# A graph layer's gather, split between GpSimd and TensorE: six instead of five of sixteen columns by matmul, with the nodes in ten sets of 625 instead of seven of 896

## The chip, the core and the metric

The kernel runs on one core of a Trainium2 chip. The metric is the device time in microseconds (us), as the median of three runs. Engines are named as in the profile: PE (TensorE; PEld is its weight load), DVE (VectorE), ACT (ScalarE), POOL (GpSimd), SP (SyncE, which issues most DMAs).

## What is computed

The layer has 6250 nodes of 64 features and 206250 edges, sorted by destination. Everything is float32.

```python
h = jnp.maximum(_layernorm(x), 0.0)
msg = relu(h[src] + edge_attr)                 # 206250 x 64
agg = segment_sum(msg, dst, num_segments=6250)
h = h + agg
h = relu(h @ W1 + b1)
return x + (h @ W2 + b2)
```

The expensive part is `h[src]`: 206250 rows of 256 bytes are picked by number.

## The kernel before

**Groups.** The edges are worked off in 201 groups of 1024 and a tail (g = 0 to 201). A group is a tile of 128 partitions by 8 columns; each column is 128 edges. For a group, `load` (L170) fetches the edge attributes `ea` by a DMA from SP's queue and the rows `xg` by one indirect DMA per column from POOL's queue (`gather`, L158). Groups 0 to 3 gather from `x` and normalise on the spot (`norm_edges`); the others gather from `h_rows`, the normalised rows that the kernel first writes to DRAM. The tiles `ea` and `xg` have `LOOK` = 10 buffers each, so group g uses the buffer of group g - 10 and its gathers wait until that group's rows have been added.

`messages` (L459) adds `xg` to `full`, a PSUM tile into which ACT has copied `ea` (`take`, L450), and applies relu on ACT (L469). `one_hot` (L437) compares destinations with slots of a window of 48 nodes on DVE, `window_sum` (L472) sums messages by destination on PE (16 matmuls in the profile for a group), and `sum_into_z` (L433) adds the sum to `z` on DVE, two groups later. Every 512 finished nodes, `hidden`, `result` and `store` apply the two dense layers, with the `rows` banks of PSUM in between.

**Columns by TensorE.** In 98 pairs of groups (k = 2 to 99, groups 2k and 2k + 1) POOL does not gather all 16 columns: the last `EVEN` = 3 columns of the even group and the last `ODD` = 2 of the odd one are gathered by matmul. The node numbers are cut into `SB` = 7 sets of `PART` = 896 nodes, each of `BB` = 7 blocks of `BN` = 128. Before the pairs begin, `ranks` (L244) gives each edge of these columns its set (`part`), its number in the set (`node`) and a slot of 128 in the set (`place`), by masks, matmuls and DVE passes for each set. For one pair, the work is:

- `hold`, `mask` (L330, L337; DVE) and `source` (L346): `T` = 5 matmuls turn this into rows that say which node stands in which slot. ACT casts them (L353), SP writes them to DRAM and reads them back as a broadcast to all partitions (`sources`, L357, 224 KB). `spot` (L359) loads the slots of the pair's edges as a broadcast (`spots`, L362).
- `find` (L365; DVE, L370): one comparison for each block makes `found`, one-hot weights from nodes to slots, 7 passes of 896 elements.
- `slots_of` (L381; PE, L386) looks the nodes up: for each set 7 matmuls of 192 columns against `hp`, the node rows in three bfloat16 pieces. Two sets share one `rows` bank. `slots_out` (L393; ACT, L394) casts them to `picked`.
- `back` (L373; DVE, L378): for each set a comparison makes `backs`, one-hot weights from slots to edges, 7 passes of 640 elements.
- `room` (L396; ACT, L403) copies the edge attributes of two columns into a `pick` bank, and `pick` (L406; PE, L412) adds to each column 7 matmuls of 192 columns, one for each set. `messages` then sums pieces and attribute (DVE, L466).

**Order.** It is written out by hand in `half(g)` (L526); each engine works its own queue in this order. In the even half of pair k, PE does for pair k + 1 the lookup of sets 0 and 1, the source matmuls of pair k + 2, the window sum of group g - 1, the lookup of sets 2 and 3 and the pick of the odd group; DVE does the messages of g, `back(k + 1)` and `mask(k + 3)`. In the odd half PE does the lookups of sets 4 to 6, the window sum, and the pick of the next even group; DVE does the messages, `find(k + 2)` and `hold(k + 3)`. ACT's order in the odd half is: cast of sets 4 and 5, relu of the messages, attributes of the next group, cast of set 6, attributes into the `pick` banks. `rows`, `pick` and `full` have two PSUM banks each.

At group 8, `find_left` looks once for edges that did not fit; a loop for them at the end of the kernel is not entered here.

Of the kernel before, what the change touches and what calls it, by code (L numbers as in the profile page):

```python
# [35 lines left out]
TN = N - NB * P * R  # L36
XC = 3
EPS = 1e-5
LOOK = 10
AHEAD = 6  # L40
LAG = 2
AB = 4


SB, BB, BN = 7, 7, 128
KB = SB * BB
PART = BB * BN
EVEN, ODD = 3, 2
T = EVEN + ODD
K0, K1 = 2, NG // 2  # L50
KS = K1 - K0
# [9 lines left out]
def kernel(  # L61
# [17 lines left out]
    const = ctx.enter_context(tc.tile_pool(name="const", bufs=1))  # L79
    edge = ctx.enter_context(tc.tile_pool(name="edge", bufs=LOOK))  # L80
    work = ctx.enter_context(tc.tile_pool(name="work", bufs=2))
# [255 lines left out]
    def mask(k):  # L337

        at = hot.tile([P, T, SB], F16, name="at", bufs=1)
        nc.vector.tensor_tensor(at, part[:, k - K0].unsqueeze(2).to_broadcast([P, T, SB]),  # L340
                                of_part.unsqueeze(1).to_broadcast([P, T, SB]), ALU.is_equal)
        mk = hot.tile([P, T, SB], F16, name="mask")
        nc.vector.tensor_tensor(mk, at, node[:, k - K0].unsqueeze(2).to_broadcast([P, T, SB]), ALU.mult)  # L343
        masks[k] = mk

    def source(k):  # L346

        oh, mk = holds.pop(k), masks.pop(k)
        ps = psum.tile([SB, P], F32, name="rows", bufs=2)
        for t in range(T):  # L350
            nc.tensor.matmul(ps, mk[:, t, :], oh[:, t, :], start=(t == 0), stop=(t == T - 1))  # L351
        col = hot.tile([SB, P], I16, name="source")
        nc.scalar.copy(col, ps)  # L353
        line = dram.tile([SB, P], I16, name="source_row", bufs=3)
        nc.sync.dma_start(out=line, in_=col)
        sources[k] = hot.tile([P, SB * P], I16, name="sources")
        nc.sync.dma_start(out=sources[k], in_=line.rearrange("(o m) s -> o (m s)", o=1).to_broadcast([P, SB * P]))  # L357

    def spot(k):  # L359

        spots[k] = hot.tile([P, T * P], BF16, name="spots")
        nc.sync.dma_start(out=spots[k], in_=spot_rows[(k - K0) * T:(k - K0 + 1) * T, :]  # L362
                          .rearrange("(o t) s -> o (t s)", o=1).to_broadcast([P, T * P]))

    def find(k):  # L365

        row = sources.pop(k)
        found[k] = hot.tile([P, BB, SB, P], BF16, name="found")
        for b in range(BB):
            nc.vector.tensor_scalar(found[k][:BN, b].rearrange("p m s -> p (m s)"), row[:BN], nodes_of[:BN, b:b + 1], None,  # L370
                                    op0=ALU.is_equal)

    def back(k):  # L373

        row = spots.pop(k).bitcast(I16)
        backs[k] = hot.tile([P, SB, T, P], BF16, name="backs")
        for m in range(SB):
            nc.vector.tensor_scalar(backs[k][:, m].rearrange("p t s -> p (t s)"), row, ids[:, m:m + 1], None,  # L378
                                    op0=ALU.is_equal)

    def slots_of(k, m, n):  # L381

        ps = psum.tile([P, 2, 3 * D], F32, name="rows", bufs=2)
        for i in range(n):
            for b in range(BB):
                nc.tensor.matmul(ps[:, i], found[k][:BN, b, m + i, :],  # L386
                                 hp[:BN, (m + i) * BB + b].rearrange("p t d -> p (t d)"),
                                 start=(b == 0), stop=(b == BB - 1))
        if m == 0:
            picked[k] = hot.tile([P, SB, 3 * D], BF16, name="picked")  # L390
        halves[k, m] = ps[:, :n]

    def slots_out(k, m, n):  # L393
        nc.scalar.copy(picked[k][:, m:m + n], halves.pop((k, m)))  # L394

    def room(g):  # L396

        m = pool_cols(g) if g < NG else G
        _, _, ea, pks = taken[g]
        for i in range(0, G - m, 2):  # L400
            n = min(2, G - m - i)
            pk = psum.tile([P, 2, 4, D], F32, name="pick", bufs=2)
            nc.scalar.copy(pk[:, :n, 3], ea[:, m + i:m + i + n])  # L403
            pks.append((pk, i, n))

    def pick(g):  # L406

        k, t0 = g // 2, EVEN if g % 2 else 0
        for pk, i, n in taken[g][3]:
            for u in range(n):  # L410
                for m in range(SB):
                    nc.tensor.matmul(pk[:, u, :3].rearrange("p t d -> p (t d)"), backs[k][:, m, t0 + i + u, :],  # L412
                                     picked[k][:, m], start=(m == 0), stop=(m == SB - 1))
# [19 lines left out]
    def sum_into_z(g):  # L433
        at = window_start(g)
        nc.vector.tensor_tensor(z[:, ds(at, W)], z[:, ds(at, W)], aggs.pop(g), ALU.add)  # L435
# [9 lines left out]
    def enter(g):  # L445
        if g <= NG and g not in taken:
            ea, xg = loaded[g] if g < RAW else load(g)
            taken[g] = [None, xg, ea, []]

    def take(g):  # L450

        if g <= NG:
            enter(g)
            n = pool_cols(g)
            full = psum.tile([P, G, D], F32, name="full", bufs=2)
            nc.scalar.copy(full[:, :n], taken[g][2][:, :n])  # L456
            taken[g][0] = full

    def messages(g):  # L459
        n, m = (G, pool_cols(g)) if g < NG else (CT, CT)  # L460
        full, xg, _, pks = taken.pop(g)
        if g < RAW:
            norm_edges(xg)
        nc.vector.tensor_tensor(full[:, :m], full[:, :m], xg[:, :m], ALU.add)  # L464
        for pk, i, c in pks:
            nc.vector.tensor_reduce(full[:, m + i:m + i + c], pk[:, :c].rearrange("p j t d -> p j d t"),  # L466
                                    AX.X, ALU.add)
        msg = work.tile([P, G, D], F32, name="msg", bufs=3)
        nc.scalar.activation(msg[:, :n], full[:, :n], AF.Relu)  # L469
        msgs[g] = msg  # L470

    def window_sum(g):  # L472
        n, oh, msg = G if g < NG else CT, hots.pop(g), msgs.pop(g)
        if g % AB == 0:
            banks.append(psum.tile([D, AB, W], F32, name="agg", bufs=1))
        pa = banks[-1][:, g % AB]
        for j in range(n):
            nc.tensor.matmul(pa, msg[:, j, :], oh[:, j, :], start=(j == 0), stop=(j == n - 1))  # L478
        aggs[g] = pa
# [34 lines left out]
    def blocks_behind(g):  # L514
        for c in sorted(res):
            store(c, *res.pop(c))
        for c in sorted(hid):
            res[c] = result(c, *hid.pop(c))
        for c in range(NB):
            if READY[c] == g:  # L520
                hid[c] = hidden(c)

    def is_set(k):
        return K0 <= k < K1

    def half(g, groups=True, sets=True):  # L526

        k, even = g // 2, g % 2 == 0
        now = sets and is_set(k + 1)
        first = (((0, 2),) if even else ((4, 2),)) if now else ()  # L530
        if groups:
            enter(g + AHEAD)
        for c in first:
            slots_of(k + 1, *c)
        if even and sets:
            if is_set(k + 2):
                source(k + 2)
            if is_set(k + 3):
                spot(k + 3)
        for c in first:  # L540
            slots_out(k + 1, *c)
        if groups:
            if g >= LAG:
                sum_into_z(g - LAG)
                blocks_behind(g - LAG)
            messages(g)
        if now and not even:
            slots_of(k + 1, 6, 1)
        if groups:
            take(g + 1)  # L550
        if now and not even:
            slots_out(k + 1, 6, 1)
        ahead = sets and g < NG and is_set((g + 1) // 2)
        if ahead:
            room(g + 1)
        if groups and g >= 1:
            window_sum(g - 1)
        if now and even:
            slots_of(k + 1, 2, 2)
            slots_out(k + 1, 2, 2)  # L560
        if ahead:
            pick(g + 1)
        if even:
            if now:
                back(k + 1)
            if sets and is_set(k + 3):
                mask(k + 3)
        elif sets:
            if is_set(k + 2):
                find(k + 2)  # L570
            if is_set(k + 3):
                hold(k + 3)
        if groups:
            one_hot(g)
        if g == 8:
            find_left()

    heads, rows = [], []
    with tc.tile_pool(name="rank", bufs=1) as rank:
# [28 lines left out]
        for g in range(2 * K0):  # L608
            half(g, sets=False)
# [36 lines left out]
    for g in range(2 * K0):  # L646
        half(g, groups=False)
    for g in range(2 * K0, NG + 1):
        half(g)
# [81 lines left out]
```

## Time and profile before

| | us |
|---|---|
| median of 3 runs (1465.42 to 1466.75) | 1465.74 |
| the profiled execution | 1465.74 |
| its span, first to last instruction | 1464.0 |
| PE busy | 1126.0 (77%) |
| PE's weight loads busy | 1029.1 (70%) |
| DVE busy | 1042.1 (71%) |
| ACT busy | 452.1 (31%) |
| POOL busy | 1103.6 (75%) |

The profile shows one execution. A group of instructions is one line, engine, operation and shape, with its count, its busy time, the mean of one and the idle time of the engine just ahead of it, with what ended that. A mean can be longer than busy time divided by the count, because one instruction starts while the one ahead of it ends; where the text counts "start to start" it goes by the first. The mean clock granted to PE is 0.881 of full speed. The DMA engines moved 140.35 MB, 96 GB/s on average. In the timeline, a line merges like instructions in a row (x21) and shows in brackets how long the engine stood idle before and what ended it.

### The profile page before, as it was taken

To read this page: it belongs to the slowest core of one execution; us is meant where nothing else is said; L and a number is where in the kernel's file an instruction comes from. 1 tells how busy PE (TensorE), PEld (TensorE's weight loads), DVE (VectorE), ACT (ScalarE), POOL (GpSimd) and SP (SyncE) were. 2 spreads that over 40 slices of the span, in tenths; PEclk is the share of its full clock that TensorE was granted. 3 is DMA by queue.
4 is the path that set the end of the run, shared out by engine and by line. 5 is a ranking of instruction groups with operands and counts; after the bars stand their busy time and mean duration, and the time that the engine had idled before them with its cause. 6 is when DMAs were issued, how large, how long until landed. Compare 5 with 4: busy or idle time off the path is not lost. (4 is left out here: it accounts for less than half of the span.)

```text
span 1464.0 us, 32135 instructions
## 1 busy us (share of the span) xinstructions
PE 1126.0 (77%) x12197; PEld 1029.1 (70%) x12197; DVE 1042.1 (71%) x2734; ACT 452.1 (31%) x1257; POOL 1103.6 (75%) x1133
## 2 busy tenths in 40 slices
PE   2419799988877886878788788787778887877874
PEld 1308788877767776777777777677767776776773
DVE  6658998986667676676776767677677676766752
ACT  3323343432232332223233232222323233223231
POOL 7777777777777777777777777777777777777774
PEclk9759999998898898888899899989999889889885
DMA  5523444543342334334343343434334334333321
GB/s 172 122 44 97 100 126 111 124 114 80 100 109 77 103 89 98 98 86 101 83 106 90 94 106 82 102 88 99 90 91 109 95 87 107 84 95 92 95 66 25
DMA packets 110196, 140.35 MB, mean 96 GB/s; under 512 B 34740, under 2 KB 66100, under 8 KB 110036
## 3 DMA queue, kind: packets, MB, share of 16 engines
q1 hardware_dynamic: 72884, 99.71, 24.5%
q0 software_dynamic: 35904, 36.84, 12.8%
q8 instruction: 97, 1.59, 0.4%
q10 hardware_dynamic: 1248, 1.70, 0.3%
q14 instruction: 63, 0.52, 0.1%
HBM read 134.64 MB, written 3.50 MB: 94 GB/s over the span
## 5 line engine op out<-in xcount | busy, mean ns | idle before, releaser
L160 POOL DMA_INDIRECT xg<-h_rows,src_sb x1090 | 1068.8, 981 | 334.1 <-issue 274.9
L412 PE MATMUL pick<-picked,backs 128*128 128x192 bf16 x3430 | 389.2, 279 | 226.9 <-ACT pick L403 226.7
L412 PEld LDWEIGHTS <-backs 128*128 128x128 bf16 x3430 | 346.1, 111 | 243.0 <-issue 224.9
L386 PE MATMUL rows<-hp,found 128*128 128x192 bf16 x4802 | 482.6, 257 | 7.1 <-DVE found L370 5.5
L386 PEld LDWEIGHTS <-found 128*128 128x128 bf16 x4802 | 422.3, 102 | 25.7 <-DVE found L370 10.7
L464 DVE TENSOR_TENSOR full<-full,xg 128x320 f32<-128x320 f32 (+1 forms) x202 | 106.9, 529 | 278.3 <-DMA xg<-h_rows,src_sb 212.0
L370 DVE TENSOR_SCALAR found<-sources,nodes_of 128x896 bf16<-128x896 int16 x686 | 260.5, 451 | 37.3 <-DMA sources<-source_row 37.3
L394 ACT CAST picked<-rows 128x384 bf16<-128x384 f32 (+1 forms) x392 | 171.0, 436 | 243.2 <-PE rows L386 243.1
L478 PE MATMUL agg<-oh,msg 128*64 128x48 f32 x3224 | 232.8, 227 | 13.6 <-ACT msg L469 8.1
L478 PEld LDWEIGHTS agg<-oh,msg 128*64 128x64 f32 x3224 | 207.4, 140 | 47.3 <-issue 25.8
L378 DVE TENSOR_SCALAR backs<-spots,ids 128x640 bf16<-128x640 int16 x686 | 222.2, 393 | 0.0
L466 DVE TENSOR_REDUCE full<-pick 128x128 f32<-128x512 f32 (+1 forms) x294 | 179.6, 611 | 50.4 <-PE pick L412 12.9
L469 ACT ACTIVATE msg<-full 128x512 f32<-128x512 f32 x202 | 119.6, 592 | 245.4 <-DVE full L466 225.2
L353 ACT CAST source<-rows 7x128 int16<-7x128 f32 x98 | 24.9, 254 | 439.9 <-PE rows L351 435.7
L440 DVE TENSOR_TENSOR oh<-slot,wslots 128x384 f32<-128x384 int16 x202 | 110.1, 545 | 0.0
L456 ACT COPY full<-ea 128x320 f32<-128x320 f32 (+1 forms) x202 | 92.5, 458 | 0.0
L333 DVE TENSOR_TENSOR holds<-place,wslots 128x640 f16<-128x640 f32 x98 | 79.6, 813 | 5.6 <-DMA spot_rows<-sp 5.6
L403 ACT COPY pick<-ea 128x128 f32<-128x128 f32 (+1 forms) x294 | 66.8, 256 | 0.0
L351 PE MATMUL rows<-holds,mask 128*7 128x128 f16 x490 | 44.1, 222 | 5.7 <-DVE mask L343 5.7
L435 DVE TENSOR_TENSOR z<-z,agg 64x48 f32 x202 | 38.3, 190 | 8.4 <-PE agg L478 5.2
L351 PEld LDWEIGHTS <-mask 128*7 128x7 f16 x490 | 25.9, 87 | 22.8 <-issue 14.8
L160 POOL DMA_INDIRECT xg<-in_x_dram,src_sb x32 | 32.9, 1028 | 11.0 <-issue 9.4
(101 smaller groups left out, 254.4 us busy)
## 6 DMA issues: line engine op xcount, KB each, us to landing
ea<-in_edge_attr_dram SPq DMA_DIRECT2D x201, 256.0 KB
sources<-source_row SPq DMA_DIRECT2D x98, 224.0 KB
xg<-h_rows,src_sb POOLq DMA_INDIRECT x1090
spots<-spot_rows SPq DMA_DIRECT2D x98, 160.0 KB
source_row<-source SPq DMA_DIRECT2D x98, 1.8 KB
x_sb<-in_x_dram SPq DMA_DIRECT2D x4, 384.0 KB
h_rows<-ln_h SPq DMA_DIRECT2D x4, 384.0 KB
h_nodes<-h_rows SPq DMA_DIRECT2D x2, 768.0 KB
```

The source lines that it names most:

```text
L160: nc.gpsimd.indirect_dma_start(out=xg[:, j, :], out_offset=None, in_=rows[:, :], in_offset=bass.IndirectOffsetOnAxis(ap=idx[:, j:j + 1], a ...
L370: nc.vector.tensor_scalar(found[k][:BN, b].rearrange("p m s -> p (m s)"), row[:BN], nodes_of[:BN, b:b + 1], None, op0=ALU.is_equal)
L378: nc.vector.tensor_scalar(backs[k][:, m].rearrange("p t s -> p (t s)"), row, ids[:, m:m + 1], None, op0=ALU.is_equal)
L386: nc.tensor.matmul(ps[:, i], found[k][:BN, b, m + i, :], hp[:BN, (m + i) * BB + b].rearrange("p t d -> p (t d)"), start=(b == 0), stop=(b ...
L394: nc.scalar.copy(picked[k][:, m:m + n], halves.pop((k, m)))
L412: nc.tensor.matmul(pk[:, u, :3].rearrange("p t d -> p (t d)"), backs[k][:, m, t0 + i + u, :], picked[k][:, m], start=(m == 0), stop=(m == ...
L440: nc.vector.tensor_tensor(oh[:, :n], slot[:, cols_of(g)].unsqueeze(2).to_broadcast([P, n, W]), wslots[:, :W].unsqueeze(1).to_broadcast([P, ...
L456: nc.scalar.copy(full[:, :n], taken[g][2][:, :n])
L464: nc.vector.tensor_tensor(full[:, :m], full[:, :m], xg[:, :m], ALU.add)
L466: nc.vector.tensor_reduce(full[:, m + i:m + i + c], pk[:, :c].rearrange("p j t d -> p j d t"), AX.X, ALU.add)
L469: nc.scalar.activation(msg[:, :n], full[:, :n], AF.Relu)
L478: nc.tensor.matmul(pa, msg[:, j, :], oh[:, j, :], start=(j == 0), stop=(j == n - 1))
```

## The change

Six of sixteen columns go by TensorE, in place of five: four of the even group and two of the odd one. The nodes are cut into ten sets of 625 (five blocks of 125) in place of seven of 896 (seven blocks of 128). So `find` makes 5 passes of 1280 elements over 125 partitions, `back` 10 passes of 768; `slots_of` does 50 matmuls, with 125 rows contracted; a column's pick has 10 matmuls; `source` has 6. POOL gathers 10 columns for a pair in place of 11. The even group's picks fill two `pick` banks, and ACT's casts are five of two sets each. In the odd half the lookups of sets 4 and 5 and of sets 6 and 7 both come first, and that of sets 8 and 9 behind the messages. The buffers of `ea` and `xg` go from 10 to 9.

```diff
-LOOK = 10
+LOOK = 9
...
-SB, BB, BN = 7, 7, 128
+SB, BB, BN = 10, 5, 125
 KB = SB * BB
 PART = BB * BN
-EVEN, ODD = 3, 2
+EVEN, ODD = 4, 2
 T = EVEN + ODD
...
         now = sets and is_set(k + 1)
-        first = (((0, 2),) if even else ((4, 2),)) if now else ()
+        first = (((0, 2),) if even else ((4, 2), (6, 2))) if now else ()
...
         if now and not even:
-            slots_of(k + 1, 6, 1)
+            slots_of(k + 1, 8, 2)
         if groups:
             take(g + 1)
         if now and not even:
-            slots_out(k + 1, 6, 1)
+            slots_out(k + 1, 8, 2)
```

## The prediction

> **What bounds the kernel now.** I read the groups of instructions first, then busy time in stretches, then the waits, then single instructions of one stretch.
>
> The group of gathers on POOL, from the page:
>
> ```profile
> L160 POOL DMA_INDIRECT xg<-h_rows,src_sb x1090 | 1068.8, 981 | 334.1 <-issue 274.9
> ```
>
> 981 ns busy and 334.1/1090 = 306 ns idle before each: POOL never waits longer than its own issue, and 1090 x 1.287 = 1403 us of 1464 are this one queue. Busy time in two stretches, early and the rest (columns: length, busy us of PE, PEld, DVE, ACT, POOL with counts, granted clock, DMA share, GB/s):
>
> ```profile
> 160.00:200.00 40.00, 38.75 (x486) 36.68 (x485) 38.28 (x105) 16.93 (x48) 30.55 (x32) 1.00 0.50 119
> 309.00:1447.00 1138.00, 904.42 (x9792) 832.86 (x9792) 787.79 (x2092) 339.37 (x980) 866.81 (x890) 0.88 0.37 93
> ```
>
> From 160 to 200 us PE is 97% busy and DVE 96%, at clock 1.00: compute is working off gathers that POOL had laid up, and a pair of groups takes 10.0 us (start to start of the messages of every second group: 161.96, 172.02, 182.01, 192.05, 202.06). After 309 us PE is 79% busy, and the waits from 400 to 1400 us say for what:
>
> ```profile
> POOL xg L160 <- issue: 194.2, 637, 0.3
> ...
> DVE full L464 <- DMA xg<-h_rows,src_sb: 170.8, 55, 6.3
> ```
>
> DVE waits for gathered rows; POOL waits for nobody. So a pair costs 11 gathers x 1.28 = 14.1 us, though compute could do it in 10.0. The compute-bound stretch is thus the measure of what the new kernel can do. One pair of it on PE, with the ACT steps ahead of its end:
>
> ```profile
> 240.40 1.89 PE L412 MATMUL pick<-picked,backs 128*128 128x192 bf16 x21 [0.49 <-ACT pick L403]
> ...
> 242.13 1.32 PE L386 MATMUL rows<-hp,found 128*128 128x192 bf16 x14
> ...
> 243.38 0.44 PE L351 MATMUL rows<-holds,mask 128*7 128x128 f16 x5
> ...
> 243.75 1.13 PE L478 MATMUL agg<-oh,msg 128*64 128x48 f32 x16
> ...
> 244.82 1.33 PE L386 MATMUL rows<-hp,found 128*128 128x192 bf16 x14
> ...
> 245.98 1.32 PE L412 MATMUL pick<-picked,backs 128*128 128x192 bf16 x14
> ...
> 247.14 1.90 PE L386 MATMUL rows<-hp,found 128*128 128x192 bf16 x21
> ...
> 248.49 0.48 ACT L394 CAST picked<-rows 128x384 bf16<-128x384 f32 x1 [1.83 <-PE rows L386]
> 248.96 1.13 PE L478 MATMUL agg<-oh,msg 128*64 128x48 f32 x16
> 248.99 0.60 ACT L469 ACTIVATE msg<-full 128x512 f32<-128x512 f32 x1
> ...
> 250.38 1.89 PE L412 MATMUL pick<-picked,backs 128*128 128x192 bf16 x21 [0.28 <-ACT pick L403]
> ```
>
> Start to start, 14 matmuls of 192 columns take 1.16 us: 83 ns each. The pair ends with a short wait (0.28) for ACT.
>
> **POOL, less.** One column of each pair goes to TensorE: 98 gathers fewer, 98 x 1.28 = 126 us. Alone this would give 1464 - 126 = 1338. It can't all be kept, for two reasons that follow.
>
> **PE, more.** Picks go from 35 (5 columns x 7 sets) to 60 (6 x 10), set lookups from 49 to 50, source matmuls from 5 to 6. I rebuild the pair above from its own pieces. Pick of the even group: 1.73 + 19 x 0.083 = 3.31. Lookup of two sets: 1.25 - 4 x 0.083 = 0.92. Source: 0.37 + 0.07 = 0.44; sums 1.07; lookup of two more 0.83; pick of the odd group 1.16 + 6 x 0.083 = 1.66. Then three lookups of two sets 2.49 + 0.07 and sums 1.07. Without waits: 8.23 + 3.63 = 11.86.
>
> Two waits for ACT, whose order the edit keeps. First, the pick of the odd group waits for its bank: source copy, cast, message, copy of attributes, copy into the bank. The same chain runs above from the source matmul (243.38); without a pause its steps are 0.54 + 0.16 + 0.48 + 0.50 + 0.40 + 0.44 = 2.52, while PE now has 0.44 + 1.07 + 0.83 = 2.34 to do: 0.18 of wait. Second, in the odd half an extra cast (sets 6 and 7) stands ahead of the message. The pick of the odd group ends at T; that lookup ends at T + 1.66; cast at + 0.19, message + 0.50, attributes + 0.49, cast of sets 8 and 9 + 0.31, bank + 0.42, pick + 0.33: T + 3.90, where PE is ready at T + 3.63: 0.27. A pair is 11.86 + 0.18 + 0.27 = 12.31.
>
> Real pairs also carry the output blocks: from 161.96 to 308.71 us 14 pairs took 146.75, or 10.48, against 10.0 undisturbed, about 0.1 of that a wait for broadcast sources. I add 0.4: **12.7 us per pair**.
>
> **DVE beside it.** Start to start before: found 0.379 each, backs 0.306, so 0.073 for 256 elements. After: 5 found of 1280 cost 0.46 to 0.48 each (2.35, was 2.65), 10 backs of 768 0.335 each (3.35, was 2.14); holds + 0.13; reductions + 0.27 (a full second bank instead of a half one); the smaller add - 0.07; masks + 0.05. From 9.6 to 10.9 of 12.7: covered, with 1.8 to spare. If that cover went, each further us per pair is 98 us.
>
> **DMA.** Broadcast sources grow from 224 to 320 KB a pair. They landed 3.3 to 4.1 us after issue; by size alone 0.6 to 1.0 more. DVE wants them 5.4 us after the source matmul, and copy, write and issue take 2.8 of it: found starts up to 2 us late. DVE's spare 1.8 and 1.2 us before its reductions hold up ACT hide it, barely; bounds 0 and 1.0 per pair, I take 0. Spots (160 to 192 KB) are loaded a half pair ahead: nothing.
>
> **POOL against DVE.** Gathers beside found lasted 1.06 us on average, beside backs 0.953, otherwise 0.94. Longer found passes: 0 to 0.05 per gather, 0 to 50 us of POOL's time, which no longer sets the end; I take 0.
> The Trainium skill (SBUF — State Buffer, Who interferes with whom) says that VectorE in a two-port mode and GpSimd exclude one another for a whole instruction. It speaks against this change, which lengthens that work; the found rows agree in kind (+ 0.12), the backs rows hardly (+ 0.01). By the rule, with every gather delayed by half a longer instruction, the sum would rise by 948 x 0.2 = 190 us on POOL, an estimate I don't use.
>
> **The start.** DVE ranks 10 sets instead of 7 (six more pairs of 0.88, fourteen pairs 0.10 longer, three masks and some passes of 588 instead of 490 elements: 9.3 us, of which 1 to 2 fall in DVE's gaps), and a fifth chunk of spots is stored (+ 1.0; 97.98 to 98.98 before). Message of group 4: 123.54 becomes about 133. POOL: before, its next gather never waited, though at 123.22 it needed the buffer just freed by group 4 (ten buffers). Now nine buffers hold groups up to 12, 44 gathers after 49.3 us, so POOL stands from about 106 to 131. Bounds: 0 to 30 us; it matters only if POOL is the bound again. Once, at group 8, DVE's pass over leftovers cost 8 us (156.37 where 148.4 was due); it stays.
>
> **The sum.** 133 + 8 + 98 x 12.7 + 13 (from the message of group 200 to the end; 16.4 before with its waits for gathers) = **1399** of span. The profiled execution took 1465.74, which is the median, for a span of 1464.0: + 1.7, so **1400 us**.
>
> **Rivals.**
> *POOL stays the bound* (20%): ACT's two waits are not there and a pair takes 12.3 or less. Then 131 + 948 gathers x 1.284 + 15 = 1363, + up to 8 from group 8: about 1370 (1355 to 1380). For: the waits are sums of short steps. Against: PE's work alone is 11.86 + 0.4.
> *Late sources stretch DVE* (18%): 0.5 to 0.7 more per pair, 1449 to 1467, say 1455. For: 25 waits for them already, 37.3 us in total. Against: DVE's spare time.
> *Slower: the 125-row lookups* (12%). The 50 lookups of a pair load weights of 125 rows instead of 128. No row shows that shape. The transposes' load of 106 columns took 170 ns, the full ones about 100; if the new loads did likewise, 50 x 0.087 = 4.3 us per pair: 1400 + 426 = 1826. It decides from 0.7 us per pair, 14 ns per lookup. Against: a load of 106 rows (group L221) took 110 ns, a full one of its kind 90 to 148. Nor does a busier PE look throttled: clock 1.00 at 97% busy.
> The Trainium skill (TensorE: Matmul & The Clock Gate, LDWEIGHTS) says that loading goes by columns, not rows; no run here shows 125 rows.
> *The forecast* has 50%, own range 1380 to 1430. That the edit does something else is no rival: the instruction order of the changed kernel shows 992 gathers from h_rows and found passes of 125x1280.
>
> **Range and chances.** 1358 to 1460 takes in the forecast, the POOL case and the smaller half of late sources; about 2 in 10 is outside. Faster by over 0.2% (what a measurement of this kernel can tell) 0.84, within 0.03, slower 0.13: the 125-row case and the far end of late sources.
>
> **What would show it.** Right: in mid-kernel PE 93% busy or more, clock near 1.00, POOL now waiting for L464 to free buffers, message to message of a pair 12.3 to 13, L403 ending PE's short waits. Wrong: gathers still at 1.28 start to start with no pause (POOL), L370 waiting for sources in most pairs (late sources), lookups over 90 ns apart (125 rows), DVE near 100%.

## The result and the profile after

The changed kernel takes 1385.93 us (median of 4 runs, 1383.09 to 1387.15) against 1466.12 for the kernel before: ratio 0.945, 95% interval 0.9434 to 0.9467. The forecast was 1400 in a range of 1358 to 1460. The profiled execution took 1385.12 us, its span is 1383.3.

The gathers on POOL, from the page, and busy time in two stretches (columns as in the prediction):

```profile
L160 POOL DMA_INDIRECT xg<-h_rows,src_sb x992 | 987.2, 995 | 334.4 <-issue 264.3
```

```profile
300.00:1200.00 900.00, 887.18 (x10871) 838.62 (x10869) 818.53 (x1987) 350.63 (x966) 688.49 (x695) 1.00 0.43 115
1200.00:1369.00 169.00, 146.49 (x1791) 137.77 (x1788) 129.82 (x312) 58.41 (x158) 129.07 (x132) 0.97 0.37 94
```

From 300 to 1200 us PE is 98.6% busy (887.18 of 900) at clock 1.00: compute sets the pace. After 1200 us PE falls to 87%. The waits from 200 to 1180 us and from 1180 to 1369 us (total, times, longest) say why:

```profile
DVE full L466 <- PE pick L412: 29.8, 52, 1.0
DVE found L370 <- DMA sources<-source_row: 27.4, 25, 2.2
```

```profile
DVE full L464 <- DMA xg<-h_rows,src_sb: 16.5, 8, 4.6
PE pick L412 <- ACT pick L403: 11.0, 8, 2.5
...
DVE full L464 <- issue: 8.9, 2, 8.1
```

At first DVE waits for PE's picks, never over 1.0 us, and for sources, never over 2.2; at the end it waits for gathered rows again, as all through the kernel before. (The 8.1 us put down to "issue" stand ahead of the addition of group 200, at 1366.11; before, the same wait, 8.1 as well, is put down to the rows.) POOL, meanwhile, stood still once, at the start. Its timeline, with its last gather:

```profile
110.47 0.94 POOL L160 DMA_INDIRECT xg<-h_rows,src_sb  x1 [0.30 <-issue]
137.35 0.94 POOL L160 DMA_INDIRECT xg<-h_rows,src_sb  x1 [25.93 <-DVE full L464]
...
1368.29 0.94 POOL L160 DMA_INDIRECT xg<-h_rows,src_sb  x1 [0.30 <-issue]
```

Up to 110.47 us POOL has gathered groups 4 to 12, all that nine buffers hold. The addition of group 4 frees one at 137. From there 948 gathers follow one another at 1.30 us, no two starts more than 3.4 apart, until the last starts at 1368.29; 15.0 us later the kernel ends. POOL's lead, from the start of a group's last gather to the addition of its rows, shrinks all the while: 50 us for group 18, 22 for group 102, 4 for group 172 (at about 1190 us). So there are two chains: PE's, which sets the pairs until about 1200 us, and POOL's, which uses up its lead by then and sets the end.

One undisturbed pair on PE, with ACT's steps ahead of its two picks:

```profile
707.83 3.46 PE L412 MATMUL pick<-picked,backs 128*128 128x192 bf16 x40
...
711.13 0.99 PE L386 MATMUL rows<-hp,found 125*128 125x192 bf16 x10
...
712.05 0.50 PE L351 MATMUL rows<-holds,mask 128*10 128x128 f16 x6
...
712.48 1.13 PE L478 MATMUL agg<-oh,msg 128*64 128x48 f32 x16
712.58 0.26 ACT L353 CAST source<-rows 10x128 int16<-10x128 f32 x1 [4.61 <-PE rows L351]
712.75 0.46 ACT L394 CAST picked<-rows 128x384 bf16<-128x384 f32 x1
...
713.12 0.58 ACT L469 ACTIVATE msg<-full 128x512 f32<-128x512 f32 x1
...
713.54 1.00 PE L386 MATMUL rows<-hp,found 125*128 125x192 bf16 x10
713.61 0.47 ACT L456 COPY full<-ea 128x384 f32<-128x384 f32 x1
714.02 0.25 ACT L403 COPY pick<-ea 128x128 f32<-128x128 f32 x1
...
714.38 1.81 PE L412 MATMUL pick<-picked,backs 128*128 128x192 bf16 x20
...
716.03 2.64 PE L386 MATMUL rows<-hp,found 125*128 125x192 bf16 x30
...
717.05 0.48 ACT L394 CAST picked<-rows 128x384 bf16<-128x384 f32 x1 [2.00 <-PE rows L386]
...
717.88 0.48 ACT L394 CAST picked<-rows 128x384 bf16<-128x384 f32 x1 [0.34 <-PE rows L386]
718.26 0.60 ACT L469 ACTIVATE msg<-full 128x512 f32<-128x512 f32 x1
...
718.60 1.13 PE L478 MATMUL agg<-oh,msg 128*64 128x48 f32 x16
...
718.75 0.39 ACT L456 COPY full<-ea 128x256 f32<-128x256 f32 x1
719.05 0.49 ACT L394 CAST picked<-rows 128x384 bf16<-128x384 f32 x1
719.42 0.48 ACT L403 COPY pick<-ea 128x128 f32<-128x128 f32 x2
...
719.76 0.41 PE L412 MATMUL pick<-picked,backs 128*128 128x192 bf16 x3
```

The next pick starts at 719.76, 11.93 us after the first (the view ends at 720 and shows three of its matmuls). No bracket stands at any PE line; brackets show waits over 0.15 us, so PE hardly waited.

### The profile page after: what moved, and what is told of

It is laid out like the page before. It is cut to its first block, busy times and chain, and to the rows that moved or that the text cites. A ratio compares the mean times of both kernels' runs of the same rounds, so it can differ in the third digit from the quotient of the medians.

```text
span 1383.3 us, 37550 instructions
## 1 busy us (share of the span) xinstructions
PE 1242.3 (90%) x14894; PEld 1163.1 (84%) x14894; DVE 1185.2 (86%) x2847; ACT 508.4 (37%) x1356; POOL 1022.5 (74%) x1035
## 4 chain that ended last, share of the span: by engine, by line
PE 61%; DMA 8%; POOL 8%; DVE 6%; issue 5%; ACT 2%; DVEq 0%; POOLq 0%; SPq 0%; ACTq 0%
PE pick L412 27%; PE rows L386 21%; PE agg L478 10%; POOL xg L160 8%; DMA xg<-h_rows,src_sb 5%; PE rows L351 2%; DVE backs L378 2%; DVE full L466 1%; DVE found L370 1%; DMA sources<-source_row 1%; PE rows L499 1%; ACT picked L394 1%; PE rows L486 1%; DMA spots<-spot_rows 1%; ACT full L456 1%
## 5 line engine op out<-in xcount | busy, mean ns | idle before, releaser
L412 PE MATMUL pick<-picked,backs 128*128 128x192 bf16 x5880 | 517.1, 246 | 23.5 <-ACT pick L403 20.7
L412 PEld LDWEIGHTS <-backs 128*128 128x128 bf16 x5880 | 488.9, 98 | 28.2 <-issue 21.4
L386 PE MATMUL rows<-hp,found 125*128 125x192 bf16 x4900 | 459.8, 247 | 6.5 <-DVE found L370 5.7
L386 PEld LDWEIGHTS <-found 125*128 125x128 bf16 x4900 | 404.8, 98 | 18.3 <-DVE found L370 7.4
L378 DVE TENSOR_SCALAR backs<-spots,ids 128x768 bf16<-128x768 int16 x980 | 335.5, 415 | 0.0
L394 ACT CAST picked<-rows 128x384 bf16<-128x384 f32 x490 | 234.3, 478 | 274.2 <-PE rows L386 269.4
L370 DVE TENSOR_SCALAR found<-sources,nodes_of 125x1280 bf16<-125x1280 int16 x490 | 251.0, 577 | 38.0 <-DMA sources<-source_row 37.6
L466 DVE TENSOR_REDUCE full<-pick 128x128 f32<-128x512 f32 x294 | 205.7, 700 | 67.5 <-PE pick L412 36.0
L464 DVE TENSOR_TENSOR full<-full,xg 128x256 f32<-128x256 f32 (+1 forms) x202 | 99.1, 491 | 33.4 <-DMA xg<-h_rows,src_sb 22.8
L333 DVE TENSOR_TENSOR holds<-place,wslots 128x768 f16<-128x768 f32 x98 | 92.4, 943 | 6.0 <-DMA spot_rows<-sp 6.0
```

Of the source, the lines that this page charges most:

```text
L386: nc.tensor.matmul(ps[:, i], found[k][:BN, b, m + i, :], hp[:BN, (m + i) * BB + b].rearrange("p t d -> p (t d)"), start=(b == 0), stop=(b ...
```

## The experiments

All times are medians; "before" is 1466.1 to 1466.6 in each comparison.

| run | what differs from the changed kernel | us | ratio to before, 95% interval |
|---|---|---|---|
| (changed) | | 1385.93 | 0.945, 0.9434 to 0.9467 |
| pick9 | PE: 6 of a pair's 60 pick matmuls left out | 1382.83 | 0.9426, 0.9411 to 0.944 |
| gather9 | POOL: 9 gathers a pair in place of 10 | 1362.61 | 0.9295, 0.928 to 0.9309 |
| look8 | 8 buffers in place of 9 | 1393.42 | 0.9504, 0.9491 to 0.9517 |
| xg11 | 11 buffers for rows, 7 for attributes | 1374.89 | 0.937, 0.9357 to 0.9383 |
| cols5 | ten sets, but 5 columns | 1480.21 | 1.0092, 1.0076 to 1.0107 |
| sets7 | 6 columns, but seven sets | 1373.36 | 0.9368, 0.9354 to 0.9382 |
| nodes2 | node loads cut in two | 1381.39 | 0.942, 0.9407 to 0.9433 |
| k0_4 | TensorE's columns from group 8 on | 1376.28 | 0.9389, 0.9376 to 0.9402 |
| cols7 | 7 columns, seven buffers | 1444.65 | 0.9846, 0.9831 to 0.9861 |
| best | nodes2, and 13 buffers for rows, 5 for attributes | 1358.83 | 0.9262, 0.9249 to 0.9274 |

**Which chain ends last: pick9 and gather9.** The first takes work from PE alone:

```diff
-                for m in range(SB):
+                for m in range(SB - 1):
                     nc.tensor.matmul(pk[:, u, :3]..., picked[k][:, m], start=(m == 0),
-                                     stop=(m == SB - 1))
+                                     stop=(m == SB - 2))
```

> Leaves out one of the ten matmuls of each pick (the tenth set), so 588 PE matmuls fewer, 6 a pair or 0.5 us a pair; POOL's gathers are as before. Theory (two chains that end almost together; POOL's ends last: from 137 us on, where group 4 frees a buffer, 948 gathers follow one another at 1.297 us, and 14 us follow the last): 1380 to 1387, because POOL's chain is untouched. Rival 1 (PE alone sets the end): 98 x 0.5 = 49 us less, about 1337.

Measured: 1382.83, 3 us less, not 49. The shorter work is there: many pairs take 11.4 us in place of 11.93. But POOL's last gather comes at 1366.2 (1368.3 in the changed kernel), and in the waits from 900 to 1369 us DVE now waits for rows much earlier:

```profile
DVE full L464 <- DMA xg<-h_rows,src_sb: 33.5, 19, 3.7
```

From the messages of group 10 to those of group 100 a pair takes 11.93 in the mean, and from there to group 200 12.91, close to POOL's ten gathers (10 x 1.295): a faster PE only meets POOL's chain sooner. So PE alone does not set the end. The second takes work from POOL alone:

```diff
+        n = pool_cols(g)
+        if g % 2 and n < G and g < NG:
+            n -= 1
+            nc.sync.dma_start(out=xg[:, n, :], in_=h_rows[g:g + P, :])
-        gather(xg, src_sb[:, cols_of(g)], pool_cols(g), x if g < RAW else h_rows)
+        gather(xg, src_sb[:, cols_of(g)], n, x if g < RAW else h_rows)
```

> In each pair one of the ten columns that POOL gathers is filled by a plain DMA of 128 neighbouring rows from SP's queue instead, with rows that are not the edge's, so POOL has 9 gathers a pair (98 x 1.297 = 127 us less) and PE the same work. Theory (two chains that end almost together): the PE chain shows alone: 139 + 8 + 98 x 12.3 to 12.4 + 13 = 1365 to 1376, so 10 to 20 us less than the changed kernel and no more. Rival 1 (PE alone sets the end): 1386, no change. Rival 2 (POOL alone): 1386 - 127 = 1259.

Measured: 1362.61, 23 us less and not 127, a little below the range given. PE's chain shows alone now: POOL starts its last gather at 1314.0, 47 us before the end, and waits for DVE to free buffers (from 300 to 1200 us; lines are 4 further down in this kernel):

```profile
POOL xg L160 <- DVE full L468: 75.6, 96, 2.4
```

From the messages of group 4 (139.3) to those of group 200 (1347.7), less the 8 us at group 8, a pair takes 12.25 us. PE's chain is thus 139.3 + 8 + 98 x 12.25 + 13.2 = 1361 of span, and POOL's, 1383, ends 22 us behind it.

**POOL's standstill: look8 and xg11.** The first is `LOOK = 8`; the second deals the 18 buffers out anew:

```diff
-        ea = edge.tile([P, G, D], F32, name="ea")
+        ea = edge.tile([P, G, D], F32, name="ea", bufs=LOOK - 2)
-        xg = edge.tile([P, G, D], F32, name="xg")
+        xg = edge.tile([P, G, D], F32, name="xg", bufs=LOOK + 2)
```

> Eight buffers in place of nine for both tiles: POOL stands still after group 11, 4 gathers or 5.2 us earlier. Theory: these are missing at the end: 1386 + 5 = 1391. Rival 1 (PE alone): 1386, no change.

> The same buffers in all (18), but 11 for gathered rows and 7 for edge attributes, in place of 9 and 9. POOL can go on to group 14 before it stands still: 10 gathers or 13 us more of its work lie ahead of group 4. Theory: POOL's chain ends at 1383 - 13 = 1370 of span, PE's at about 1373, so 1373 to 1378 in time. Rival 1 (PE alone): 1386. Rival 2 (POOL alone): 1373.

Measured: 1393.42 and 1374.89, 7.5 more (5 expected) and 11 less. The standstill moved with the buffers and the end with the standstill; first look8, then xg11:

```profile
137.60 0.94 POOL L160 DMA_INDIRECT xg<-h_rows,src_sb  x1 [31.67 <-DVE full L464]
```

```profile
138.80 0.94 POOL L160 DMA_INDIRECT xg<-h_rows,src_sb  x1 [15.50 <-DVE full L464]
```

**The two halves of the change: cols5 and sets7.** `EVEN, ODD = 3, 2` in the changed kernel, and `LOOK = 9`, `EVEN, ODD = 4, 2` in the kernel before:

> Ten sets of 625 nodes, but 5 of 16 columns by TensorE as before the change (3 and 2), so POOL has 11 gathers a pair again. Theory: POOL gathers groups 4 to 12 (49) and stands still until about 136 us; then 1041 x 1.29 + 14: 1493, so 1485 to 1503 in time, slower than before the change, since PE's and DVE's extra work for ten sets buys nothing by itself and nine buffers make POOL wait. Rival (the set count and the buffers cost nothing): 1466.

> The kernel before with 6 of 16 columns by TensorE (4 and 2) and nine buffers, seven sets of 896 as before. 495 of its 75264 edges find no slot of 128 in their set; they are left out (the loop for leftovers is not entered). PE has 42 picks and 49 lookups a pair, about 10.6 us. Theory: POOL alone sets the end: it resumes at about 124 us, 948 gathers x 1.285 + 14 = 1356, so 1352 to 1366 in time; the ten sets thus cost 20 to 30 us and are there to make the edges fit. Rival (the ten sets cost nothing): 1386.

Measured: 1480.21, slower than before by 0.9%, as the theory has it, but 5 us under its range; and 1373.36, 7 us over its range. Ten sets with nine buffers buy nothing by themselves. The whole gain is the column: with both, 11 gathers a pair give 1480, 10 give 1386. With seven sets POOL resumes at 126.9 in place of 137.35, which is 10 of the 13 us between sets7 and the changed kernel; PE's extra picks (PE is 89% busy in sets7 from 300 to 1200 us, 797.20 of 900) lie beside POOL's work. What ten sets buy is room: counted in the edge list, 495 edges of 75264 overflow seven sets, and none overflows ten.
Most of both misses is POOL's pace: I had used 1.29 us a gather for cols5 and 1.285 for sets7; it is 1.280 and 1.296, which is some 10 us each. The rest is the end of the standstill: 132.6 where about 136 was expected, and 126.9 for 124. See the last section.

**The set-up: nodes2.**

```diff
-                nc.sync.dma_start(out=h[:BN, :n], in_=h_rows[...].rearrange("(k p) d -> p k d", p=BN))
+                rows = h_rows[...].rearrange("(k p) d -> p k d", p=BN)
+                nc.sync.dma_start(out=h[:112, :n], in_=rows[:112])
+                nc.sync.dma_start(out=h[112:BN, :n], in_=rows[112:])
```

> Each load of node rows into 125 partitions is cut in two, 112 and 13 partitions. In the changed kernel these loads moved at 104 to 113 GB/s, where 128 partitions had 214 to 231 before, and ACT waited 6.4 us for them in the set-up. Theory: the rate comes from the 125 partitions; the cut brings it back, the pairs start 4 to 6 us earlier and the end comes as much earlier: 1380 to 1382. Rival (the rate has another cause): 1386.

Measured: 1381.39, 4.5 us less, inside the theory's range. The messages of group 4 come at 132.2 in place of 139.2, 7 us earlier where 4 to 6 were expected, and ACT's wait of 6.4 us for these loads is gone. The DMA in the stretch of the loads (the last two columns: busy share of the 16 DMA engines, and GB/s of all traffic), in the kernel before, in the changed kernel and then cut in two:

```profile
64.00:71.00 7.00, 1.97 (x19) 1.84 (x18) 3.72 (x9) 1.09 (x2) 5.48 (x6) 0.50 1.27 226
```

```profile
81.00:93.00 12.00, 1.29 (x19) 1.01 (x16) 9.03 (x20) 3.46 (x7) 9.26 (x10) 0.74 0.45 98
```

```profile
81.00:92.00 11.00, 1.13 (x16) 1.01 (x16) 9.49 (x20) 3.97 (x7) 8.26 (x10) 0.74 1.08 166
```

**A later start: k0_4** (`K0, K1 = 4, NG // 2`).

> TensorE's columns begin at group 8 in place of 4 (96 pairs), so POOL gathers groups 4 to 7 whole: 12 gathers more, done in the 26 us in which it stood still. Theory: POOL never stands still: 49 + 1004 x 1.297 + 14 = 1365; PE's chain: pairs start at about 152, 152 + 8 + 96 x 12.4 + 13 = 1363. So 1365 to 1376. Rival 1 (PE alone): 2 pairs fewer and a later start, about 1365 as well. Rival 2 (POOL's work alone, standstill or not): 12 x 1.297 = 16 us more, 1402.

Measured: 1376.28, 10 us less, 0.3 above the theory's range. In the profiled execution, the slowest of the five with 1380.14, POOL's standstill shrank from 27 to 5 us and not to nothing, and 12 gathers more (16 us) must be done.

**The other side of the balance: cols7** (`EVEN, ODD = 4, 3`, `LOOK = 7`).

> The changed kernel with 7 of 16 columns by TensorE (4 and 3), ten sets, seven buffers; 50 edges that find no slot in their set are left out (the loop for leftovers is not entered). POOL has 9 gathers a pair, PE ten picks and a source matmul more: 11.93 + 0.9 = 12.8 undisturbed, 13.2 with the 0.4 that the one-gather-less kernel showed on top. Theory (PE's chain sets the end as soon as POOL's is short): 142 + 8 + 98 x 13.2 + 13 = 1457, so 1445 to 1470, where the gain is given back. Rival (POOL still decides): 1386 - 127 = 1259, or up to 1300 with the standstill of fewer buffers.

Measured: 1444.65, 0.35 us below the range. An undisturbed pair takes 12.8 us as worked out, PE is 99% busy from 300 to 1300 us (991.24 of 1000), and POOL waits for PE's pace:

```profile
POOL xg L160 <- DVE full L464: 134.7, 149, 3.4
```

With five columns POOL is the bound, with seven PE is; with six their chains end 22 us apart.

**Both repairs: best.** The node loads of nodes2 with 13 and 5 buffers, and `AHEAD = 4`, so that attributes are loaded 4 groups ahead.

> The changed kernel with the node loads cut in two and the same 18 buffers dealt out as 13 for gathered rows and 5 for edge attributes (loaded 4 groups ahead in place of 6). POOL can go on to group 16. Theory: the standstill of 27 us shrinks to about 0 to 4, POOL's last gather comes at 1342 to 1348, and 15 us follow: 1357 to 1365; PE's chain, 1361 in the one-gather-less kernel, starts 7 us earlier and ends at 1354, so it still comes second. Rival (only the buffers or only the loads count): 1370 to 1376.

Measured: 1358.83, inside the theory's range, and faster than both kernels: 0.9262 of before. In the profiled execution (1361.34) POOL's standstill is gone: its longest step from one gather to the next is 4.6 us, at 47 us, where it goes over from `x` to `h_rows`, and its last gather comes at 1344.55.

## Why the prediction was right, and where it was not

**The bound moves to PE: right until about 1200 us.** PE is 98.6% busy at clock 1.00, which the prediction read off 40 us of the kernel before. Matmuls keep their 83 ns: the ten lookups from 711.13 to 712.05 take 0.92, the forty picks from 707.83 to 711.13 take 3.30 (0.92 and 3.31 forecast). DVE is 91% busy there (818.53 of 900), so it was covered, as forecast.

**ACT's two waits (0.18 + 0.27 per pair): wrong.** An undisturbed pair is 11.93, near the 11.86 without waits and not 12.31. From the source matmul to the pick of the odd group it is 2.33 (712.05 to 714.38) in place of 2.52, and PE's own work fills it: the step from cast to message was priced too high (0.48; now 0.37, 712.75 to 713.12), and so was the last one, from bank to pick (0.44; now 0.36 at most, 714.02 to 714.38). In the pair of the kernel before that these steps were read from, the message waited for DVE:

```profile
244.02 0.46 ACT L394 CAST picked<-rows 128x384 bf16<-128x384 f32 x1
...
244.64 0.60 ACT L469 ACTIVATE msg<-full 128x512 f32<-128x512 f32 x1 [0.16 <-DVE full L466]
```

The forecast took the pause of 0.16 out, but where nothing holds the message it also starts 0.09 before the cast ends (713.12 against 712.75 + 0.46). And the 0.44 from bank to pick (245.54 to 245.98) was no step of ACT's: PE was still at its lookups until then. In the odd half, counted from T = 716.03, cast to message is 0.38 and cast to bank 0.37 where 0.50 and 0.42 were forecast; the chain lets the pick start at T + 3.73, where PE was to be ready at T + 3.63, so at most 0.1 of wait is left. A pair of 11.93 in place of 12.31 is 98 x 0.38 = 37 us of PE's chain, the largest mis-sized term. What pairs carry on top was 12.25 - 11.93 = 0.32 in gather9; 0.4 was forecast. Late sources cost little: 27.4 us of waits in 980 us, beside DVE's spare time.

**POOL "no longer sets the end": wrong.** The prediction expected POOL to wait for buffers in mid-kernel. After 175 us it never did for longer than its own issue (0.3 us), as its pairs take 13.0 us (10 x 1.30) and PE's 12.25. The prediction's own prices say as much: 10 x 1.284 = 12.84 for POOL against 12.7 for PE. It compared the ends of the two chains, where POOL's was 36 us ahead, but not these two paces. The sign that it had named for the rival, gathers with no pause, is what the trace shows. The rival "POOL stays the bound" (20%) had the right condition (a pair of 12.3 or less), the right chain and two terms too small: the resumption (131, measured 137.35: 6 us) and the pace (1.284, measured 1.30: 15 us over 948 gathers).

**The start: too short by 6 us.** 133 was forecast for the messages of group 4; they came at 139.16. The longer ranking was priced right: the messages of group 3 moved from 81.44 to 89.19, 7.75 later (9.3 less 1 to 2 forecast). The loads of node rows were left out: cut in two (nodes2) they let the messages of group 4 come 7 earlier.

**The forecast of 1400 is close because two errors offset.** PE's chain was put at 1399 and is 1361 (37 less for ACT's waits, 98 x 0.08 = 8 less for what pairs carry, 6 more for the start); the chain that ends last was put at 1363 and is 1383. That 1400 lies 14 us from the measured time is luck: by its own terms, rightly sized, the chain that it added up ends 22 us too early.

**The 125-row rival fell.** The lookups' weight loads of 125 rows take 98 ns in the mean, like those of 128 rows in the picks:

```profile
L412 PEld LDWEIGHTS <-backs 128*128 128x128 bf16 x5880 | 488.9, 98 | 28.2 <-issue 21.4
...
L386 PEld LDWEIGHTS <-found 125*128 125x128 bf16 x4900 | 404.8, 98 | 18.3 <-DVE found L370 7.4
```

**The clock.** Before, the granted clock was 0.88 after 309 us, with waits of PE for ACT up to 6.5 us; now it is 1.00 from 300 to 1200 us, where these waits go up to 1.3. The Trainium skill (TensorE: Matmul & The Clock Gate, Part 1: The HAM clock gate) says that the clock halves after an idle window of some 3.4 us and comes back under sustained work; the rows agree in kind. PE was not the bound before; what the higher clock is worth by itself was not tried.

## What to carry to other kernels

When work moves from one engine to another, write down both chains from their start to the end and compare the sums: the pace that sets most of the steps need not be the one that ends last, and a lead of a few buffers hides this for a long time. A producer that stands still once, at the start, pays for it at the end if it is the later chain; deal out buffers by what each tile needs. Where a forecast wait is the small difference of two long chains, as ACT's were here, an error of a tenth of a microsecond in each step decides whether it is there at all.

## What the runs showed of the hardware that was not expected

**The loads into 125 partitions were slow.** The first load of node rows (781 KB) was issued at 81.23 us and let ACT start at 92.42, at 98 GB/s with all other traffic; before, two loads of 768 KB into 128 partitions moved at 226 GB/s (64 to 71 us). Cut into 112 and 13 partitions the loads came up to 166. The cut also makes four DMAs of two, but the kernel before had two as well, so their number is not the cause. The Trainium skill (DMA: Bandwidth & Descriptors, Why a DMA increments its semaphore by 16 and not by 1) says that a DMA is spread over the largest number of engines up to 16 that divides the slowest dimension of both its ends. By that rule 125 partitions would use 5 engines and 112 all 16. The traces do not show which engine moved what, but their packets agree: of the loads' queue 6 were under way at a time in the mean (83 to 101 us), against 21 before (65 to 71 us) and 20 with the loads cut (83 to 90 us); as an estimate, 6/21 of 16 engines is 4.6. The loads also started 18 us later than before (81.23 against 62.96): in both kernels SP's queue waits for PE's last matmul of the ranking (`pick`, L270; 28.2 us and 13.2), and the ranking now goes through ten sets. What that costs by itself was not tried.

**Gathers lengthen beside longer passes of `backs`, hardly of `found`.** I sorted the gathers from 200 to 1200 us by what DVE ran 0.75 us after their start. Beside `backs` passes of 640 elements they last 0.953 us (before) and 0.963 (cols5), beside passes of 768 1.003 (changed) and 1.000 (sets7). Beside `found`, passes of 896 give 1.059 (before) and 1.054 (sets7), passes of 1280 1.063 (changed) and 1.072 (cols5). POOL's pace from 200 to 1200 us is 1.281 (before), 1.280 (cols5), 1.297 (changed) and 1.296 (sets7): it goes with the `backs` size, and neither with the `found` size nor with the number of sets. The two kernels with 640 elements also have 11 gathers a pair and those with 768 have 10, so a pair's DVE work falls on fewer gathers; the two were not separated.
